# Layer 2's product with the squared adjacency: exact 12-bit halves in three single-pass products in place of Strassen's seven fp32 products

## The chip, the cores and the metric

The kernel runs on one core of one Trainium2 chip. The metric is the device time of one execution in microseconds (us). Engine names are those of the profile: PE (TensorE, with PEld for its weight loads), DVE (VectorE), ACT (ScalarE), POOL (GpSimd), SP (SyncE, which here only issues DMAs).

## The reference, cut to what matters

Four layers run one after the other on `x` (32 x 512 x 128, fp32), each as `x = x + layer(relu(layernorm(x)))`. Layer 2 is the one concerned:

```
weights  = coeff * A                       # both are adj: the squared adjacency, 512 x 512
features = relu(H @ psi_w + psi_b)         # H = relu(layernorm(x))
messages = einsum('nm,bnd->bmd', weights, features)
h        = relu(concat(messages, H) @ phi1_w + phi1_b)
x        = x + h @ phi2_w + phi2_b
```

The line `messages` is the product that the change rewrites: for each of the 32 batch entries, a 512 x 512 matrix (transposed) by a 512 x 128 one. Layer 0 (softmax attention), layer 1 (two Chebyshev hops) and layer 3 (tanh-limited attention masked by `adj`) stay as they are.

## The kernel before, in words

**Tiling.** Tokens lie in four blocks of 128 partitions (`NT` = 4). A *round* `q` handles two batch entries at once, so there are 16 rounds per layer (`NQ` = 16). All products are in fp32. One fp32 matmul in the program shows as two LDWEIGHTS and two MATMUL records in the trace: `p_score` is issued 128 times by the loops of lines 1089 to 1110 (16 rounds, two entries, four blocks) and has 256 records.

**The product with Strassen.** `mixed` (line 393) computes the product of the 512 x 512 matrix with the two entries of a round by a seven-product form of Strassen's scheme in which the two entries and the two halves of the token axis make the 2 x 2 blocks. Each of the seven products is `by_feature` (line 376): two matmuls that hold a 128 x 128 block of features and stream 256 columns of the matrix, so a round has 14 matmuls and 28 records. The left operands need three sums of the matrix's blocks, made once by `sum_steps` (line 301) and kept in a tile with the tag `sums` (two buffers). The right operands need four differences of 128 x 256 per round, made on POOL by `right_blocks` (line 338) in tiles of the tag `rt` (six buffers of 128 x 512). Three PSUM banks, a, c and d, take the products; two ACT copies and five DVE additions per round carry them out (lines 400 to 419).

**Layer 2.** `layer2(q)` (line 1053) is a generator whose parts are: normalise (ACT), transpose through DVE and a bounce in DRAM, one idle part, features (`p_feat` on PE, bias on DVE, Relu on ACT, then the right operands), the product `p_msgT` and four small POOL additions of `phi2b`, `p_phi`, and last `p_l2` with the addition into `x`. Its messages go to `msgT`.

**The squared matrix.** `square()` (line 1139) loads `adj` into the tile `sq` with its rows crossed, loads the transposed mask `adjTx` for layer 3, squares the four blocks on POOL with a copy back, and makes the block sums. `sq` and `adjTx` each take one of the four buffers of the tag `square`, which also hold `adj_s`, `x1T` and, in layer 3, the tiles `ex`.

**Order of the work.** Up to line 1157 (layer 0) the order on PE, DVE, ACT and POOL is as written. After it, the loop of lines 1166 to 1172 advances all active generators by one part per step, oldest first; a new round enters in each step. In one step PE thus gets, from the oldest round to the newest, `p_l2`, `p_phi`, `p_msgT` and `p_feat` of four neighbouring rounds. This order is the priority from which the framework's planner lays out each engine's queue and hands out buffers: an instruction whose tile has no free buffer is held back. Layer 1's last two pairs of rounds overlap layer 2's first rounds and use the same `rt` tiles; layer 2's last rounds overlap layer 3's first.

Of the kernel before, what the change touches and what calls it, by code (L numbers as in the profile page):

```python
# [8 lines left out]

F32 = mybir.dt.float32  # L10
F16 = mybir.dt.float16
BF16 = mybir.dt.bfloat16
AF = mybir.ActivationFunctionType
OP = mybir.AluOpType
AX = mybir.AxisListType

P = 128
QR = 32
NQR = P // QR
NEG = 9000000000000000.0  # L20
EPS = 1e-5


@with_exitstack
def kernel(
# [37 lines left out]
    nc = tc.nc  # L63
    B, N, D = x.shape
    NT = N // P
# [4 lines left out]
    const = ctx.enter_context(tc.tile_pool(name="const", bufs=1))  # L70
# [3 lines left out]
    work = ctx.enter_context(tc.tile_pool(name="work", bufs=4))  # L74
    bounce = ctx.enter_context(tc.tile_pool(name="bounce", bufs=4, space=bass.MemoryType.DRAM))

    def bank(name):
        return psum.tile([P, 512], F32, tag="bank", name=name)

# [7 lines left out]
    def square_tile(name):  # L87
        return const.tile([P, NT, N], F32, tag="square", name=name, bufs=4)

    def crossed(ap):  # L90

        return ap.rearrange("p (a b c) -> p b a c", a=NT, b=NQR)

    def split(ap):
        return ap.rearrange("p (a b c) -> p a b c", a=NT, b=NQR)

    def load_crossed(dst, src):
        for b in range(NQR):
            tc.keep_in_program_order(
                nc.sync.dma_start(dst[:, b, :], src.rearrange("(a b c) w -> b a c w", a=NT, c=QR)[b]))  # L100
# [91 lines left out]
    shift, scale = {}, {}  # L192
# [105 lines left out]
    H = N // 2  # L298
    sums = {}

    def sum_steps(mat, name, eng=nc.gpsimd):

        a11, a12 = mat[:, 0:2, 0:H], mat[:, 2:4, 0:H]
        a21, a22 = mat[:, 0:2, H:N], mat[:, 2:4, H:N]
        extra = const.tile([P, 3, 2, H], F32, tag="sums", name=f"sums_{name}", bufs=2)
        s1, s2, s4 = extra[:, 0], extra[:, 1], extra[:, 2]
        sums[name] = {1: a11, 2: a12, 3: s4, 4: a22, 5: s1, 6: s2, 7: a21}
        for out, op, p, q in ((s1, OP.add, a21, a22), (s2, OP.subtract, s1, a11),
                              (a21, OP.subtract, a11, a21), (s4, OP.subtract, a12, s2)):
            tc.keep_in_program_order(eng.tensor_tensor(out, p, q, op))  # L310
            yield
# [6 lines left out]
    def att_sums():  # L318

        a11, a12 = attT[:, 0:2, 0:H], attT[:, 2:4, 0:H]  # L320
        a21, a22 = attT[:, 0:2, H:N], attT[:, 2:4, H:N]
        extra = const.tile([P, 3, 2, H], F32, tag="sums", name="sums_att", bufs=2)
        s1, s2, s4 = extra[:, 0], extra[:, 1], extra[:, 2]
        sums["att"] = {1: a11, 2: a12, 3: s4, 4: a22, 5: s1, 6: s2, 7: a21}
        yield
        for out, p, bank_of, half, first in ((s1, a21, 2, 1, False), (s2, s1, 0, 0, False),
                                             (a21, a21, 0, 0, True), (s4, s2, 2, 0, True)):
            for k in range(2):
                b = pt[bank_of + k][:, half * H : half * H + H]
                if out is s1:  # L330
                    nc.vector.tensor_add(out[:, k], b, p[:, k])
                elif first:
                    nc.vector.tensor_sub(out[:, k], b, p[:, k])
                else:
                    nc.vector.tensor_sub(out[:, k], p[:, k], b)
            yield

    def right_blocks(half, name, engs):

        right = {}  # L340
        for _ in right_steps(half, name, engs, right):
            pass
        return right
# [21 lines left out]
    def products(name, form, left, right, evict, order=ORDER, on=lambda k, p: p):  # L365


        banks = {}
        for k, g, first in order:
            if first:  # L370
                banks[g] = bank(f"p_{name}_{g}")
            form(on(k, banks[g]), left[k], right[k], first)
            evict(k, banks[g])
            yield
# [18 lines left out]
    def mixed(name, left, right, dst):  # L393

        m1 = dst[:, 0, H:], dst[:, 1, :H], dst[:, 1, H:]

        def evict(k, p):
            p = p[:, :H]
            if k == 1:
                nc.scalar.copy(m1[0], p)  # L400
            elif k == 6:
                nc.vector.tensor_add(m1[1], p, m1[0])
            elif k == 7:
                nc.vector.tensor_add(m1[2], p, m1[0])
            elif k == 5:
                return
            elif k == 2:
                nc.scalar.copy(dst[:, 0, :H], p)
            elif k == 4:
                nc.vector.tensor_add(dst[:, 0, H:], p, m1[0])  # L410
            elif k == 3:
                nc.vector.tensor_add(dst[:, 1, :H], p, m1[1])

        def evict2(k, p):
            evict(k, p)
            if k == 5:
                held.append(p)
            if k == 7:
                nc.vector.tensor_add(dst[:, 1, H:], held[0][:, :H], m1[2])

        held = []
        return products(name, by_feature, left, right, evict2)

    def at(hT, b):
        return lambda t: hT[:, t, b, :]
# [90 lines left out]
    for t in range(NT):  # L516
        for s in range(t + 1):
            nc.tensor.matmul(pi[:, t : t + 1], upto[:, s, blk(t)], rch[:, s : s + 1],
                             start=(s == 0), stop=(s == t))

    p = bank("p_qk_t")
# [27 lines left out]
    parts = []  # L549
    for i in range(3):  # L550
        eh = prep.tile([P, NK], BF16, name=f"eh_{i}")
        nc.gpsimd.tensor_copy(eh, ecoln)
        part = prep.tile([P, NK], F32, name=f"part_{i}")
# [11 lines left out]
    for t in range(NT):  # L565
        s = prep.tile([P, NE], F16, tag="lt", name=f"lt_{t}", bufs=2)
# [3 lines left out]
        for j in range(NT):  # L570
            nc.tensor.matmul(pg[j // 2][:, j % 2, :], m[:, t, blk(j)], of_row[:, t, :],
                             start=(t == 0 and j % 2 == 0), stop=(t == NT - 1), skip_group_check=True)
    pb = bank("p_known")[:, : 2 * NK].rearrange("p (k e) -> p k e", e=2)
    for kk in range(NK):
        for t in range(NT):
            nc.tensor.matmul(pb[:, kk, :], of_row[:, t, blk(kk)], known[:, t, :],
                             start=(t == 0), stop=(t == NT - 1))
# [17 lines left out]
    for kk in range(NK):  # L595
        for j in range(NT):
            nc.tensor.matmul(pw[kk][:, j * P :], pgs[:, j, blk(kk)], upto[:, j, j * P :],
                             start=(j == 0), stop=(j == NT - 1), skip_group_check=True)
# [10 lines left out]
    for kk in range(NK):  # L609
        s = prep.tile([P, N], F16, tag="scr", name=f"scr_c{kk}", bufs=2)  # L610
# [88 lines left out]
    late = ctx.enter_context(tc.tile_pool(name="late", bufs=4))  # L699
# [338 lines left out]
    def layer1_stats():  # L1038

        ln_stats(NQ - 2)  # L1040
        yield
        ln_stats(NQ - 1)
# [10 lines left out]
    def layer2(q):  # L1053
        h = normed(q)
        yield
        hT = transposed(h, f"hT2_{q}")
        yield
        yield
        feat = []
        for b in range(2):  # L1060
            pf = projected(f"p_feat_{q}_{b}", (at(hT, b), psi))
            feat.append(late.tile([P, NT, D], F32, tag="hs", name=f"feat_{q}_{b}", bufs=6))
            nc.vector.tensor_add(feat[b], pf, spread(psib, NT))  # L1063
            nc.scalar.activation(feat[b], feat[b], AF.Relu)  # L1064
        right = right_blocks(lambda J, b: feat[b][:, 2 * J : 2 * J + 2, :], f"feat_{q}", [nc.gpsimd] * 4)
        yield
        if q % 2 == 0:
            msgs.append(quad_tile(f"msgT_{q}"))
        msgT = msgs[-1][:, q % 2, : 2 * N].rearrange("p (b w) -> p b w", b=2)
        for _ in mixed(f"msgT_{q}", sums["sq"], right, msgT):  # L1070
            pass
        for b in range(2):
            for i in range(0, NT, 2):
                xi = xt[q][:, b, i : i + 2, :]
                tc.keep_in_program_order(nc.gpsimd.tensor_add(xi, xi, spread(phi2b, 2)))  # L1075
        yield
        h1T = msgT
        for b in range(2):
            ph = bank(f"p_phi1_{q}_{b}")
            nc.tensor.matmul(ph, phi1[:, 1, :], hT[:, :, b, :], start=True, stop=False)  # L1080
            nc.tensor.matmul(ph, phi1[:, 0, :], msgT[:, b], start=False, stop=True)
            nc.scalar.activation(crossed(h1T[:, b]), split(ph), AF.Relu, bias=phi1b)
        yield
        for b in range(2):
            po = projected(f"p_l2_{q}_{b}", (columns(h1T[:, b]), phi2))
            nc.vector.tensor_add(xt[q][:, b], po, xt[q][:, b])
        ln_stats(q)
# [46 lines left out]
            if not final:  # L1134
                nc.sync.dma_start(out_r, xt[q][:, b])

    adjTx = []

    def square():

        sq = square_tile("sq")
        load_crossed(sq, adj)
        adjTx.append(square_tile("adjTx"))
        load_crossed(adjTx[0], adjT_d)
        yield
        for i in range(NT):
            s = late.tile([P, N], F32, tag="hs", name=f"sq_{i}", bufs=6)
            nc.gpsimd.tensor_mul(split(s), crossed(sq[:, i, :]), crossed(sq[:, i, :]))
            nc.gpsimd.tensor_copy(sq[:, i, :], s)
        yield from sum_steps(sq, "sq")  # L1150

    next_layer = layer1(0)
    for r in range(NQ // 2):
# [4 lines left out]
    waiting = [[next_layer, layer1(1), layer0_stats()]]  # L1158
# [3 lines left out]
    waiting[-1].append(layer2(0))  # L1162
    waiting += [[layer2(q)] for q in range(1, NQ)]
    waiting[-NQ + 7].append(layer1_stats())
    waiting += [[layer3(q)] for q in range(NQ)]
    active = []
    while waiting or active:
# [37 lines left out]
```

## Time and profile before

| | before |
|---|---|
| time, median of three (us) | 963.71 (963.55 to 964.28) |
| span of the profiled execution (us) | 961.7 |
| PE busy, records | 953.3 us (99%), 5465 |
| DVE busy | 584.4 us (61%) |
| ACT busy | 469.1 us (49%) |
| POOL busy | 423.8 us (44%) |
| DMA | 86.04 MB, mean 89 GB/s |

"Busy" is the union of the time in which an engine has an instruction in work. PE's matmuls overlap one another[...], so the duration of one record is longer than its share of PE: what a matmul costs a full PE is read from the distance between the *starts* of neighbouring records. The timeline gives, for a run of like records, the start of the first and their number, and so this distance.

The records of `p_msgT` run from 451.3 us to 670.2 us of the span. This is layer 2's stretch, and its first 20 us overlap layer 1.

### The profile page before, as it was taken

How to read it: one execution, taken by the hardware profiler on the slowest of the kernel's cores; microseconds unless marked ns; L12 is line 12 of the kernel's file. 1: busy time of each engine (PE TensorE's matmuls, PEld its weight loads, DVE VectorE, ACT ScalarE, POOL GpSimd, SP SyncE). 2: the span in 40 equal slices, each digit the busy share in tenths (PEclk: the TensorE clock that was granted, in tenths of full speed). 3: DMA queues.
4: the chain of work that ended last, by engine and by line, in shares of the span. 5: the costliest groups of instructions: out<-in, count | busy, mean ns of one | idle time of the engine just before them, and what ended most of it. 6: DMA issues, size and time to landing. Idle time of an engine off the chain costs nothing.

```text
span 961.7 us, 15152 instructions
## 1 busy us (share of the span) xinstructions
PE 953.3 (99%) x5465; PEld 780.8 (81%) x5465; DVE 584.4 (61%) x1326; ACT 469.1 (49%) x1054; POOL 423.8 (44%) x470
## 2 busy tenths in 40 slices
PE   8999999999999999999999999999999999999998
PEld 4899999898989999899877777777677777767776
DVE  8888885846536545656667665665654444444444
ACT  5865542442232233277627655444765445544553
POOL 5878987833517522513333444433032233223322
PEclk9999999999999999999999999999999999999999
DMA  9356532441341230343333433223121121211111
GB/s 252 62 166 185 160 108 84 104 110 55 102 136 45 66 88 23 110 110 96 89 99 97 126 91 85 74 82 88 56 88 56 55 77 44 72 61 45 55 33 44
DMA packets 83913, 86.04 MB, mean 89 GB/s; under 512 B 6784, under 2 KB 74624, under 8 KB 83840
## 3 DMA queue, kind: packets, MB, share of 16 engines
q1 hardware_dynamic: 83552, 84.57, 31.6%
q8 instruction: 43, 0.70, 0.3%
q10 hardware_dynamic: 288, 0.52, 0.2%
q14 instruction: 30, 0.25, 0.1%
HBM read 44.17 MB, written 40.89 MB: 88 GB/s over the span
## 4 chain that ended last, share of the span: by engine, by line
PE 96%; ACT 2%; DVE 1%; DMA 0%; POOL 0%; issue 0%; DVEq 0%; ACTq 0%
PE p_av L1125 12%; PE p_score L1110 11%; PE p_l_c L386 8%; PE p_w L435 6%; PE p_l_d L386 6%; PE p_msgT_c L379 5%; PE p_l_a L386 4%; PE p_x1T_c L379 4%; PE p_l L435 3%; PE p_feat L435 3%; PE p_hv L435 3%; PE p_qkh L1097 3%; PE p_x1T_a L379 3%; PE p_msgT_d L379 3%; PE p_g L435 3%; PE p_x1T_d L379 3%
## 5 line engine op out<-in xcount | busy, mean ns | idle before, releaser
L247 ACT ACTIVATE h<-x,sh,rs 128x128 f32<-128x128 f32 x512 | 209.2, 484 | 51.7 <-PE p_x1T_d L379 21.7
L1115 POOL TENSOR_TENSOR ex<-ex,adjTx 128x512 f32<-128x512 f32 x62 | 80.3, 1295 | 208.3 <-ACT ex L1113 202.8
L1111 ACT ACTIVATE ex<-p_score 128x512 f32<-128x512 f32 x128 | 71.9, 587 | 122.8 <-issue 113.0
L1125 PEld LDWEIGHTS p_av<-qkh_hv,ex 128*128 128x128 f32 x1024 | 118.4, 191 | 8.4 <-issue 7.4
L1125 PE MATMUL p_av<-qkh_hv,ex 128*128 128x129 f32 x1024 | 119.9, 274 | 0.0
L1110 PE MATMUL p_score<-qkh_hv,hT 128*128 128x512 f32 x256 | 115.2, 593 | 0.0
L283 DVE STREAM_TRANSPOSE hb_hT<-h 128x512 f32<-128x512 f32 x120 | 82.0, 698 | 23.7 <-ACT h L247 22.6
L1115 DVE TENSOR_TENSOR ex<-ex,adjTx 128x512 f32<-128x512 f32 x66 | 46.1, 703 | 82.0 <-ACT ex L1113 81.9
L227 DVE BATCH_NORM_STATS2 bn<-x 128x6 f32<-128x256 f32 x248 | 89.8, 419 | 0.6
L1110 PEld LDWEIGHTS p_score<-qkh_hv,hT 128*128 128x128 f32 x256 | 46.2, 190 | 46.5 <-issue 44.5
L1113 ACT ACTIVATE ex<-ex 128x512 f32<-128x512 f32 x128 | 76.7, 630 | 1.9
L356 POOL TENSOR_TENSOR rt_feat<-feat,feat 128x256 f32<-128x256 f32 x16 | 11.6, 725 | 136.4 <-ACT feat L1064 136.4
L958 ACT COPY w<-p_w 128x512 f32<-128x512 f32 x32 | 18.2, 574 | 106.1 <-PE p_w L435 106.1
L356 POOL TENSOR_TENSOR rt_w<-w,rt_w 128x512 f32<-128x512 f32 x16 | 20.4, 1273 | 110.3 <-DVE rt_w L356 92.0
L435 PE MATMUL p_w<-th,x1T 128*128 128x128 f32 x256 | 49.5, 275 | 0.0
L435 PE MATMUL p_w<-th,hs 128*128 128x128 f32 x256 | 49.5, 275 | 0.0
L435 PEld LDWEIGHTS p_hv<-vw,hT 128*128 128x128 f32 x256 | 33.6, 192 | 15.3 <-issue 8.1
L1075 POOL TENSOR_TENSOR x<-x,phi2b 128x256 f32<-128x256 f32 x64 | 44.5, 727 | 0.0
L435 PEld LDWEIGHTS p_w<-th,hs 128*128 128x128 f32 x256 | 39.9, 192 | 0.7
L1064 ACT ACTIVATE feat<-feat 128x512 f32<-128x512 f32 x32 | 20.1, 629 | 41.4 <-DVE feat L1063 41.4
L1130 DVE SCALAR_TENSOR_TENSOR x<-p_av,rsum,x 128x128 f32<-128x128 f32 x128 | 39.1, 347 | 1.9
L712 POOL TENSOR_TENSOR hd<-hT,adiag 128x512 f32<-128x512 f32 x32 | 39.6, 1274 | 0.2 <-ACT adiag L838 0.2
(238 smaller groups left out, 2039.7 us busy)
## 6 DMA issues: line engine op xcount, KB each, us to landing
d_hT<-hb_hT SPq DMA_DIRECT2D x240, 128.0 KB
hT<-d_hT SPq DMA_DIRECT2D x60, 512.0 KB
x<-in_x_dram SPq DMA_DIRECT2D x32, 256.0 KB
out_dram<-x SPq DMA_DIRECT2D x31, 256.0 KB
adjT_d<-adj_squares SPq DMA_DIRECT2D x4, 256.0 KB
sq<-in_adj_dram SPq DMA_DIRECT2D x4, 256.0 KB
adjTx<-adjT_d SPq DMA_DIRECT2D x4, 256.0 KB
adj_s<-in_adj_dram ACTq DMA_DIRECT2D x2, 256.0 KB
```

The costliest lines, as they stand in the source:

```text
L227: nc.vector.bn_stats(st[:, k].rearrange("p e s -> p (e s)"), xt[q][:, b, t : t + 2, :].rearrange("p t f -> p f t"))
L247: nc.scalar.activation(h[:, b, t, :], xt[q][:, b, t, :], AF.Relu, bias=shift[q][:, i : i + 1], scale=scale[q][:, i : i + 1])
L283: nc.vector.transpose(hb[:, :, b].rearrange("p j t r -> p t j r"), h[:, b].rearrange("p t (j c) -> p t j c", c=QR))
L379: nc.tensor.matmul(p[:, :H], b[:, k, :], a[:, k, :], start=(first and k == 0), stop=(k == 1), skip_group_check=True)
L386: nc.tensor.matmul(p[:, i * 2 * D : (i + 1) * 2 * D], a[:, k, blk(i)], b[:, k], start=(first and i == 0 and k == 0), stop=(k == 1), skip_g ...
L435: nc.tensor.matmul(p[:, blk(t)], hT(t), w, start=(i == 0), stop=(i == len(terms) - 1))
L1075: tc.keep_in_program_order(nc.gpsimd.tensor_add(xi, xi, spread(phi2b, 2)))
L1110: nc.tensor.matmul(ps, hT[:, t, b, :], qkh, start=True, stop=True)
L1111: nc.scalar.activation(ex[:, t, :], ps, AF.Tanh, scale=1.0 / (8.0 * math.sqrt(D)))
L1113: nc.scalar.activation(ex[:, t, :], ex[:, t, :], AF.Exp, scale=8.0)
L1115: eng.tensor_mul(split(ex[:, t, :]), split(ex[:, t, :]), crossed(adjTx[0][:, t, :]))
L1125: nc.tensor.matmul(po[:, i, : D + 1], ex[:, t, blk(i0 + i)], hv[:, t, :], start=(t == 0), stop=(t == NT - 1))
```

## The change

The seven products are replaced by three. A matrix `a` is split into `high`, its value rounded to a short significand (a write into the 32-bit type `float32r`, after a factor just under 1), and the rest. With the rest as `low` and a third part `mid` that combines both, the sum of three products of parts gives the full product. Each part is meant to be held exactly in 12 bits, so that a matmul on `float32r` operands can take it in a single pass. The three products are plain: all 512 columns of the matrix stream past each 128 x 128 block of the features, four blocks per product, for each of the two entries (24 matmuls per round). `near` collects high and low, `far` the mid part. ACT carries `near` out with a factor, and DVE adds `far`.

- `right_parts` splits the features of an entry: one pass of 128 x 512 each on ACT, POOL and DVE per entry, in place of the four POOL differences of 128 x 256 per round. It takes three `rt` tiles per entry, six per round, where the Strassen differences took two per round.
- `left_parts` splits the squared matrix once, block by block. `sq_high` and `sq_low` take two `square` buffers, and `sq_mid` one of `sums`, whose buffers grow from three to four parts.
- `square` now loads `adj` row block by row block through tiles of the tag `hs`, with a yield after each load and each block.
- The load of `adjTx` moves from `square` to `load_mask`, which enters with the last but one round of layer 2.

```diff
-        extra = const.tile([P, 3, 2, H], F32, tag="sums", name=f"sums_{name}", bufs=2)
+        extra = const.tile([P, 4, 2, H], F32, tag="sums", name=f"sums_{name}", bufs=2)
...
+    def left_parts(src, parts, i):
+        high, low, mid = (part[:, i, :] for part in parts)
+        nc.scalar.activation(high, src, AF.Copy, scale=DOWN)
+        nc.gpsimd.tensor_sub(src, src, high.bitcast(F32))
+        nc.scalar.activation(low, src, AF.Copy, scale=LOW)
+        nc.gpsimd.tensor_sub(mid, low.bitcast(F32), high.bitcast(F32))
+
+    def right_parts(src, name):
+        high, low, mid = (work.tile([P, NT, D], F32R, tag="rt", name=f"{part}_{name}", bufs=6)
+                          for part in ("high", "low", "mid"))
+        nc.scalar.activation(high, src, AF.Copy, scale=DOWN)
+        nc.gpsimd.tensor_sub(low, src, high.bitcast(F32))
+        nc.vector.scalar_tensor_tensor(mid, high.bitcast(F32), UP, src, OP.mult, OP.subtract)
+        return high, low, mid
+
+    def mixed_parts(name, left, right, dst):
+        near, far = bank(f"p_{name}_near"), bank(f"p_{name}_far")
+        for p, part in ((near, 0), (near, 1), (far, 2)):
+            for t in range(NT):
+                nc.tensor.matmul(p, right[part][:, t, :], left[part][:, t, :],
+                                 start=(t == 0 and part != 1), stop=(t == NT - 1 and part != 0))
+            if part == 1:
+                nc.scalar.activation(dst, near, AF.Copy, scale=UP)
+        nc.vector.tensor_add(dst, far, dst)
...
-        right = right_blocks(lambda J, b: feat[b][:, 2 * J : 2 * J + 2, :], f"feat_{q}", [nc.gpsimd] * 4)
+        right = [right_parts(feat[b], f"feat_{q}_{b}") for b in range(2)]
...
-        for _ in mixed(f"msgT_{q}", sums["sq"], right, msgT):
-            pass
+        for b in range(2):
+            mixed_parts(f"msgT_{q}_{b}", sq, right[b], msgT[:, b])
...
     def square():
-        sq = square_tile("sq")
-        load_crossed(sq, adj)
+        sq.extend(const.tile([P, NT, N], F32R, tag="square", name=f"sq_{part}", bufs=4) for part in ("high", "low"))
+        sq.append(const.tile([P, NT, N], F32R, tag="sums", name="sq_mid", bufs=2))
+        adj_b = adj.rearrange("(a b c) w -> b a c w", a=NT, c=QR)
+        for i in range(NT):
+            row = late.tile([P, N], F32, tag="hs", name=f"adj_{i}", bufs=6)
+            tc.keep_in_program_order(nc.sync.dma_start(row, adj_b[i]))
+            yield
+            s = late.tile([P, N], F32, tag="hs", name=f"sq_{i}", bufs=6)
+            nc.gpsimd.tensor_mul(split(s), crossed(row), crossed(row))
+            left_parts(s, sq, i)
+            yield
+
+    def load_mask():
+        yield
         adjTx.append(square_tile("adjTx"))
         load_crossed(adjTx[0], adjT_d)
-        yield
-        for i in range(NT):
-            s = late.tile([P, N], F32, tag="hs", name=f"sq_{i}", bufs=6)
-            nc.gpsimd.tensor_mul(split(s), crossed(sq[:, i, :]), crossed(sq[:, i, :]))
-            nc.gpsimd.tensor_copy(sq[:, i, :], s)
-        yield from sum_steps(sq, "sq")
...
+    waiting[-2].append(load_mask())
```

More of the change, by code (lines that the diff above doesn't have):

```diff
@@ L10 @@
 F32 = mybir.dt.float32
+F32R = mybir.dt.float32r
 F16 = mybir.dt.float16
@@ L21 @@
 EPS = 1e-5
+LOW = 4096.0
+DOWN = 1.0 - 1.0 / 8192.0
+UP = 1.0 + 1.0 / 4096.0
 @with_exitstack
@@ L321, in att_sums @@
         a21, a22 = attT[:, 0:2, H:N], attT[:, 2:4, H:N]
-        extra = const.tile([P, 3, 2, H], F32, tag="sums", name="sums_att", bufs=2)
+        extra = const.tile([P, 4, 2, H], F32, tag="sums", name="sums_att", bufs=2)
         s1, s2, s4 = extra[:, 0], extra[:, 1], extra[:, 2]
@@ L1135, in layer3 @@
                 nc.sync.dma_start(out_r, xt[q][:, b])
-    adjTx = []
+    adjTx, sq = [], []
     def square():
-        sq = square_tile("sq")
-        load_crossed(sq, adj)
+        sq.extend(const.tile([P, NT, N], F32R, tag="square", name=f"sq_{part}", bufs=4) for part in ("high", "low"))
[11 more added lines that the diff above has]
+        yield
         adjTx.append(square_tile("adjTx"))
         load_crossed(adjTx[0], adjT_d)
-        yield
-        for i in range(NT):
-            s = late.tile([P, N], F32, tag="hs", name=f"sq_{i}", bufs=6)
-            nc.gpsimd.tensor_mul(split(s), crossed(sq[:, i, :]), crossed(sq[:, i, :]))
-            nc.gpsimd.tensor_copy(sq[:, i, :], s)
-        yield from sum_steps(sq, "sq")
     next_layer = layer1(0)
```

## The prediction

> **What bounds the kernel now.** I began with the page's first two parts, the busy times and the slices.
>
> ```profile
> PE 953.3 (99%) x5465; PEld 780.8 (81%) x5465; DVE 584.4 (61%) x1326; ACT 469.1 (49%) x1054; POOL 423.8 (44%) x470
> ...
> PE   8999999999999999999999999999999999999998
> ```
>
> PE is busy in every slice, and no other engine is over 61%. The share alone doesn't say that PE streams all the time, so next came the chain of work that ended last:
>
> ```profile
> PE 96%; ACT 2%; DVE 1%; DMA 0%; POOL 0%; issue 0%; DVEq 0%; ACTq 0%
> ```
>
> 96% of the way back from the end is PE itself. What is taken from PE comes off the time one for one, as long as nothing else takes the place. What the product costs on PE is seen in the timeline of PE over one round of layer 2:
>
> ```profile
> 610.69 1.03 PE L379 MATMUL p_msgT_a<-sq,feat 128*128 128x256 f32 x4
> 611.56 1.03 PE L379 MATMUL p_msgT_c<-sums_sq,rt_feat 128*128 128x256 f32 x4
> 612.42 1.03 PE L379 MATMUL p_msgT_d<-sums_sq,rt_feat 128*128 128x256 f32 x4
> 613.41 1.13 PE L379 MATMUL p_msgT_c<-sq,rt_feat 128*128 128x256 f32 x4
> 614.38 1.03 PE L379 MATMUL p_msgT_a<-sq,feat 128*128 128x256 f32 x4
> ...
> 616.97 1.95 PE L435 MATMUL p_feat<-psi,hT 128*128 128x128 f32 x16
> 618.75 1.95 PE L435 MATMUL p_l<-phi,msgT 128*128 128x128 f32 x16
> 620.54 1.02 PE L1080 MATMUL p_phi<-hT,phi 128*128 128x512 f32 x2
> ...
> 623.98 1.03 PE L379 MATMUL p_msgT_a<-sq,feat 128*128 128x256 f32 x4
> ```
>
> Columns: start, length, engine and line, names, shapes, number of records. Four records take 611.56 - 610.69 = 0.865 us, that is 0.216 us each. The 28 records of the product take 616.97 - 610.69 = 6.28 us: 28 x 0.216 = 6.05, and two small gaps (0.99 instead of 0.865 before 613.41, 0.97 before 614.38), together 0.23 us. The whole round is 623.98 - 610.69 = 13.29 us: product 6.28, `p_feat` 1.78, `p_l` 1.79, `p_phi` 3.44. Last, what the product's prepared operands wait for, in the view of the tile `rt_feat`:
>
> ```profile
>   ACT feat L1064: 136.4, 16
>   DVE msgT L402: 4.5, 12
> ```
>
> POOL idles before each of the 16 rounds, because features come late, not because POOL is full. The second line shows what the small gaps are: in 12 rounds a PSUM bank is freed by DVE just too late.
>
> **What the Trainium skill says.** "FP8 and Floating Point Precision", TensorE Precision Notes: true FP32 takes four passes, while the reduced-precision way reads the 4-byte value, truncates it and multiplies natively. The trace agrees with the four: one fp32 matmul of 256 columns is 2 x 0.216 = 0.432 us, and 4 x 256 columns at the page's 2.4 GHz are 0.427. No record of before is of the reduced kind. "TensorE: Matmul & The Clock Gate", Back-to-back issue gap, prices an isolated pass at N/2.4 + 2.5 ns, so 0.216 us for 512 columns. Before has bf16 matmuls of that width, and they agree (6 in 21.29 - 20.00 = 1.29 us, 0.215 each):
>
> ```profile
> 20.00 1.46 PE L635 MATMUL p_val<-at_part,at_row 128*128 128x512 bf16 x6
> 21.29 0.59 PE L631 MATMUL p_later<-at_col,at_row 128*128 128x512 bf16 x2
> ```
>
> The same page, LDWEIGHTS, puts a load at columns/1.2, so 107 ns. Here a 4-byte load lasts 0.19 us, but 16 of them pass in 1.97 us (0.12 each) under `p_feat`, so one per 0.216 us is hidden. And in its section on the array it calls ACT and DVE strict FIFOs: an instruction that waits holds what is queued behind it.
>
> **The change part by part.**
>
> *The product on PE.* 24 matmuls of 512 columns replace 28 records. The cost of one `float32r` record is not in the trace. From below it is one pass, 0.216 us (the bf16 row); from above it is what a fp32 record of that width takes, `p_phi`, 3.44/8 = 0.430 us, since each fp32 record streams two cycles a column. I take 0.216, since the count of four passes fits the measured fp32 matmul to 1%, and a reduced operand needs one. A round's product is then 24 x 0.216 = 5.18 us, and 16 rounds give 16 x (6.05 - 5.18) = 13.9 us. The two gaps should go as well: `near` takes eight matmuls without an eviction in between, and `far` has its own bank. 12 rounds x 0.23 = 2.8 us. PE gains 16.7 us.
>
> *Evictions.* ACT loses two copies of 128x256 (0.357 + 0.369) and gets two of 128x512 (0.58, the row of `w<-p_w`). DVE loses five additions of 0.42 = 2.10 us and gets two of 0.69 = 1.38. `p_phi` reads the messages only after `p_feat` and `p_l` of neighbouring rounds, 3.6 us of PE work; the last addition ends under 1 us after the last matmul. At nothing.
>
> *Splitting the features.* Per round: ACT two more copies at 0.63 (the row of Relu on `feat`), POOL two subtractions at 1.27 in place of four at 0.727 (2.54 for 2.91), DVE two `scalar_tensor_tensor` at 0.68 to 0.80 (the two rows of line 996; I take 0.80). Sums per round: ACT +1.70, DVE +0.88, POOL -0.37 us. In 600 to 680 us, the undisturbed part of layer 2, ACT is busy 38.2 and DVE 47.5 of 80 us, so 6.3 and 7.9 of a round of 13.29. They become 8.0 and 8.8 of 12.2: 66% and 72%. Neither bounds.
>
> The new waits: `low` on POOL and `mid` on DVE wait for `high` on ACT, which waits for the Relu. Behind `mid` on DVE stand the additions of `p_l` and layer 1's or 2's statistics; behind `high` on ACT the next Relu and the normalisation of a round three steps ahead, which no one needs yet. From the end of `p_feat`'s first entry to its use lies the second entry (0.9), `p_l` (1.79) and `p_phi` (3.44), 6.1 us. The chain is DVE bias 0.69 + Relu 0.63 + `high` 0.63 + `low` 1.27 = 3.2 us, up to 5 with some 0.2 to 0.4 us of hand-over at each step and one foreign instruction in the way. `low` is wanted only four matmuls later still. Hidden in the steady state.
>
> *Buffers.* A round now needs all six `rt` tiles, where it took two. In the steady state a round's tiles are free once its product has run, before the next is split. Where layer 1's last pairs overlap, four tiles of `rt_w` and six of parts must take turns: pair 6's products, round 0, pair 7's, round 1. After three such turns one chain of about 3 us may be bare, though PE has `p_w` (7 us between 436 and 451) and others to put there. I charge 2 us; bounds 0 and 10.
>
> *Once.* Squaring: POOL 4 x 1.15 + 8 x 1.27 = 14.8 us against 4 x 1.15 + 4 x 0.72 + 4 x 1.27 = 12.6; ACT + 8 x 0.63 = 5 us; spread over nine steps of layer 1, where POOL is at half. `adjTx` is 1 MB, fetched two rounds before its use at 26% DMA share, into a buffer left by layer 1. Both at nothing.
>
> Sum: 963.7 - 13.9 - 2.8 + 2 = 949.0 us.
>
> **The rivals.**
> - *The preparation takes part of it back.* For it: the six buffers all used, a chain through three strict queues, and the loads of `adj` through `hs` in SP's queue, ahead of other rounds' transfers. Against: PE has at least 5 us of other work in each round. Three bare turns at 3.2 us, and nothing of the small gaps gained: 963.7 - 13.9 + 9.6 = 959.4.
> - *A `float32r` record streams two cycles a column.* For it: the fp32 transposes in layer 0 (`p_hT`, eight in 23.89 - 23.02 = 0.87 us, one record each) take 0.109 us for 128 columns, twice a pass, so 4-byte operands may be fed at half rate. Against: a transpose has to carry all 32 bits. Then 384 x 0.430 = 165.1 against 96.8 + 2.8: 963.7 + 65.5 = 1029, slower.
> - *The chain is bare in every round*, by 2 us, because `mid` is stuck in DVE behind statistics: 949 + 32 = 981, slower. Against it stand the 6.1 us.
>
> **How the numbers follow.** My forecast 0.70, partly taken back 0.17, two cycles 0.08, bare each round 0.05. The forecast reaches from 945 (no loss at the turns, and a little more regained) to about 954; of the second case most lies below 961, and a fifth or so (0.03) within 0.2% of before. The range 945 to 961 thus leaves out the two slow cases and that fifth. Faster 0.70 + 0.14 = 0.84, same 0.03, slower 0.13.
>
> **What would show it.** Records of `p_msgT` 0.216 us apart, 384 of them; a steady round of 12.2 us; no gap in PE before `near` or `far`; ACT and DVE at about 66% and 72% there. PE idle before the first rounds of layer 2 would show the turns of the `rt` tiles. A distance of 0.43 us would refute the step "a reduced operand needs one pass"; a wait on `low` or `mid` in the list of PE's waits would refute "hidden".

## The result, and the profile after

| | before | after |
|---|---|---|
| time, median (us) | 963.82 (963.55 to 964.28) | 968.62 (967.46 to 969.72) |
| ratio to before, 95% interval | | 1.005 (1.0036 to 1.0064) |
| span of the profiled execution (us) | 961.7 | 966.6 |
| PE busy (us) | 953.3 | 945.7 |

The change is slower by 4.8 us, where 14.7 us of gain were forecast. The page of the changed kernel, busy times and slices:

```profile
PE 945.7 (98%) x5401; PEld 771.1 (80%) x5401; DVE 602.1 (62%) x1310; ACT 496.9 (51%) x1094; POOL 436.8 (45%) x438
...
PE   8999999999996999999999999999999999999998
...
PEclk9999999999998999999999999999999999999999
```

PE is busy for 7.6 us less, and yet the span is longer. The 13th slice has a 6 where PE stood at 9 before, and the granted clock dips beside it. The chain that ended last says the same; it was 96% PE before:

```profile
PE 79%; POOL 9%; issue 6%; DMA 2%; DVE 2%; ACT 2%; POOLq 0%; DVEq 0%
```

The list of PE's waits (who waited for whom, total us, times, longest) names the place:

```profile
PE p_x1T_c L383 <- DVE x1T L406: 12.1, 4, 8.7
...
PE p_msgT_near L453 <- POOL low_feat L444: 0.7, 1, 0.7
```

`p_x1T` is layer 1's product, which the diff doesn't touch. Before, this wait (line 402 there) came to 0.2 us. What the change was about, the product `p_msgT`, has one wait of 0.7 us in 16 rounds. A round of layer 2 in the timeline of PE:

```profile
605.89 1.02 PE L1116 MATMUL p_phi<-msgT,phi 128*128 128x512 f32 x2
606.35 1.50 PE L453 MATMUL p_msgT_near<-sq_high,high_feat 128*128 128x512 f32 x4
607.68 1.10 PE L453 MATMUL p_msgT_near<-sq_low,low_feat 128*128 128x512 f32 x4
608.61 1.10 PE L453 MATMUL p_msgT_far<-sq_mid,mid_feat 128*128 128x512 f32 x4
609.55 1.09 PE L453 MATMUL p_msgT_near<-sq_high,high_feat 128*128 128x512 f32 x4
...
612.34 1.95 PE L470 MATMUL p_feat<-psi,hT 128*128 128x128 f32 x16
...
618.95 1.49 PE L453 MATMUL p_msgT_near<-sq_high,high_feat 128*128 128x512 f32 x4
```

Four records take 608.61 - 607.68 = 0.93 us, so 0.233 us each, and the groups follow one another without a gap. (The first `near` record starts under the last `p_phi` record, whose pair takes 0.86 us elsewhere; so the product has 612.34 - 606.75 = 5.59 us, which is 24 x 0.233.) The round is 618.95 - 606.35 = 12.60 us, against 13.29 before. Layer 2 did become faster. Added up over the 16 rounds, from the first record to what follows, the products took 99.9 us before and take 90.8 now, a gain of 9.1 us. Twelve rounds take 5.57 to 5.60 us; four take 5.67, 6.52, 5.84 and 5.67, and in the last three of these a group of `low` is late. The loss lies in layer 1, around 300 us, where the squared matrix is split. PE's timeline there:

```profile
300.64 1.03 PE L383 MATMUL p_x1T_d<-sums_adj,rt_h 128*128 128x256 f32 x4
310.40 2.07 PE L383 MATMUL p_x1T_c<-adj_s,rt_h 128*128 128x256 f32 x4 [8.73 <-DVE x1T L406]
312.27 1.66 PE L383 MATMUL p_x1T_a<-adj_s,h 128*128 128x256 f32 x4
313.76 1.03 PE L383 MATMUL p_x1T_c<-adj_s,rt_h 128*128 128x256 f32 x4
```

PE stands still for 8.73 us. The eight records after it take 313.76 - 310.40 = 3.36 us instead of 8 x 0.216 = 1.73, so 1.6 us more are lost to a slow clock. The Trainium skill, "TensorE: Matmul & The Clock Gate", Part 1, says that an idle window of about 3.4 us drops the PE clock to half until it has been busy as long; the trace agrees: the mean granted clock is 0.53 in these 3.36 us, and 1.00 in 320 to 340 us. DVE's addition of line 406 waits for ACT's copy of line 404, and ACT's timeline shows why that is late:

```profile
299.58 0.63 ACT L436 ACTIVATE sq_low<-sq 128x512 fp32r<-128x512 f32 x1 [2.31 <-POOL sq L435]
300.12 0.57 ACT L993 COPY w<-p_w 128x512 f32<-128x512 f32 x1
300.58 0.50 ACT L237 ACTIVATE sd<-bn,eps 128x8 f32<-128x8 f32 x2
307.00 0.63 ACT L434 ACTIVATE sq_high<-sq 128x512 fp32r<-128x512 f32 x1 [5.92 <-POOL sq L1184]
307.53 0.57 ACT L993 COPY w<-p_w 128x512 f32<-128x512 f32 x1
309.00 0.63 ACT L436 ACTIVATE sq_low<-sq 128x512 fp32r<-128x512 f32 x1 [0.90 <-POOL sq L435]
309.53 0.35 ACT L404 COPY x1T<-p_x1T_a 128x256 f32<-128x256 f32 x1
```

The copy of line 404, whose matmuls were done by about 300 us, stands in ACT's queue behind `sq_high` and `sq_low` of the second block. These wait for POOL, and POOL waits for the row of `adj`:

```profile
305.93 1.04 POOL L1184 TENSOR_TENSOR sq<-adj 128x512 f32<-128x512 f32 x1 [4.37 <-DMA adj<-in_adj_dram]
```

That load was issued at 300.23 us and landed 5.56 us later. What held the issue is in SyncE's timeline, and in the list of its waits:

```profile
300.23 0.57 SPq L1181 DMA_DIRECT2D adj<-in_adj_dram  x1
```

```profile
SPq L1181 <- ACT w L993: 7.8, 1, 7.8
```

The issue had waited 7.8 us, in the end for ACT: its copy `w` stood behind the first block's `sq_low`, which had waited 2.31 us for POOL and ended at 300.21 us, just before the issue. So the row is late in part because ACT's queue was blocked already. Two of the other three waits, at 348.77 (1.58 us) and 385.67 (1.63 us), have the same chain from the row on.

### The profile page after: what moved, and what is told of

Its sections match the earlier page's. It is cut to its first block, busy times and chain, and to the rows that moved or that the text cites. A ratio compares the mean times of both kernels' runs of the same rounds, so it can differ in the third digit from the quotient of the medians.

```text
span 966.6 us, 15066 instructions
## 1 busy us (share of the span) xinstructions
PE 945.7 (98%) x5401; PEld 771.1 (80%) x5401; DVE 602.1 (62%) x1310; ACT 496.9 (51%) x1094; POOL 436.8 (45%) x438
## 4 chain that ended last, share of the span: by engine, by line
PE 79%; POOL 9%; issue 6%; DMA 2%; DVE 2%; ACT 2%; POOLq 0%; DVEq 0%
PE p_av L1160 12%; PE p_score L1145 11%; PE p_l_c L390 6%; PE p_w L470 4%; PE p_x1T_c L383 4%; PE p_msgT_near L453 4%; PE p_l_d L390 4%; PE p_l_a L390 3%; PE p_hv L470 3%; PE p_qkh L1132 3%; PE p_x1T_a L383 3%; PE p_x1T_d L383 3%; PE p_msgT_far L453 2%; PE p_g L470 2%; PE p_l L470 2%
## 5 line engine op out<-in xcount | busy, mean ns | idle before, releaser
L444 POOL TENSOR_TENSOR low_feat<-feat,high_feat 128x512 fp32r<-128x512 f32 x32 | 52.6, 1658 | 119.4 <-ACT high_feat L443 114.1
L237 ACT ACTIVATE sd<-bn,eps 128x8 f32<-128x8 f32 x62 | 18.5, 304 | 61.6 <-DVE bn L231 54.6
L1110 POOL TENSOR_TENSOR x<-x,phi2b 128x256 f32<-128x256 f32 x64 | 47.8, 778 | 0.0
L383 PE MATMUL p_x1T_c<-adj_s,rt_h 128*128 128x256 f32 x128 | 34.9, 396 | 12.1 <-DVE x1T L406 12.1
L453 PE MATMUL p_msgT_near<-sq_high,high_feat 128*128 128x512 f32 x128 | 40.8, 440 | 0.0
```

Of the source, the lines that this page charges most:

```text
L383: nc.tensor.matmul(p[:, :H], b[:, k, :], a[:, k, :], start=(first and k == 0), stop=(k == 1), skip_group_check=True)
L453: nc.tensor.matmul(p, right[part][:, t, :], left[part][:, t, :], start=(t == 0 and part != 1), stop=(t == NT - 1 and part != 0))
```

## The experiments

My theory after the result: PE is held through ACT's queue, by work of the squaring that waits for POOL, and with the late rows as the root. Rivals: POOL or the loads alone hold PE; or the chain of the splitting does so whether rows are late or not.

**Rows early.** The changed kernel, with the four blocks of `adj` loaded together into a free `quad` tile, one step before the first is squared:

```diff
-        for i in range(NT):
-            row = late.tile([P, N], F32, tag="hs", name=f"adj_{i}", bufs=6)
-            tc.keep_in_program_order(nc.sync.dma_start(row, adj_b[i]))
-            yield
+        rows = quad_tile("adj_rows").rearrange("p w e -> p (w e)")[:, : 4 * N].rearrange("p (t w) -> p t w", t=NT)
+        for i in range(NT):
+            tc.keep_in_program_order(nc.sync.dma_start(rows[:, i, :], adj_b[i]))
+        yield
+        for i in range(NT):
+            row = rows[:, i, :]
             s = late.tile([P, N], F32, tag="hs", name=f"sq_{i}", bufs=6)
```

> The changed kernel with one edit: the four row blocks of adj are loaded together, one step before the first is squared, into a free quad tile instead of one by one through hs tiles. Theory (late rows: POOL waits in order for a row that was issued late and takes 5.5 us to land, ACT's sq_high and sq_low wait behind it, and the x1T eviction behind those holds PE): PE's 12.1 us of waits on DVE x1T L406 go below 2 us, with them about 2 us of slow PE clock; 953 to 957 us. Rival (the splitting chain itself, ACT to POOL to ACT, is what delays the eviction, whenever the row is there): the waits stay above 8 us; 964 to 969 us.

Measured: 962.88 us, ratio to before 0.9993 (0.9985 to 1.0002). PE's waits there:

```profile
PE p_x1T_c L383 <- DVE x1T L406: 6.4, 2, 6.2
```

This is neither number. With no row missing, 6.4 of the 12.1 us stay, all but 0.2 in one wait, at 307.74 us. ACT's timeline shows the queue once more, now with two blocks' parts ahead of the copy:

```profile
305.85 0.63 ACT L436 ACTIVATE sq_low<-sq 128x512 fp32r<-128x512 f32 x1 [0.42 <-POOL sq L435]
306.39 0.57 ACT L993 COPY w<-p_w 128x512 f32<-128x512 f32 x1
306.85 0.38 ACT L404 COPY x1T<-p_x1T_a 128x256 f32<-128x256 f32 x1
```

So the late row is part of the cause, not its root: POOL's own queue (here `rt_h`, `hs` and the splitting of two blocks) is enough to hold ACT. The edit also takes out a `yield` per block, so that blocks follow one step apart and not two, and two of them meet here; how much of the 6.4 us one block alone would leave isn't shown.

**The row loads alone.** The kernel before, with Strassen, and the squares made from rows that are loaded as in the change:

```diff
         sq = square_tile("sq")
-        load_crossed(sq, adj)
         adjTx.append(square_tile("adjTx"))
         load_crossed(adjTx[0], adjT_d)
-        yield
+        adj_b = adj.rearrange("(a b c) w -> b a c w", a=NT, c=QR)
         for i in range(NT):
+            row = late.tile([P, N], F32, tag="hs", name=f"adj_{i}", bufs=6)
+            tc.keep_in_program_order(nc.sync.dma_start(row, adj_b[i]))
+            yield
             s = late.tile([P, N], F32, tag="hs", name=f"sq_{i}", bufs=6)
-            nc.gpsimd.tensor_mul(split(s), crossed(sq[:, i, :]), crossed(sq[:, i, :]))
+            nc.gpsimd.tensor_mul(split(s), crossed(row), crossed(row))
             nc.gpsimd.tensor_copy(sq[:, i, :], s)
+            yield
```

> The kernel before (Strassen) with the row by row loading of the change alone: each block of adj through an hs tile, squared and copied into sq on POOL in the step after; nothing of it on ACT. If a late row needs ACT to reach PE (theory): POOL waits for rows, PE idles under 3 us more than before; 964 to 967 us. If POOL's wait alone reaches PE through rt_h or hs (rival): 970 to 976 us.

Measured: 963.47 us, ratio 0.9999 (0.9991 to 1.0008), and PE waits as before (0.2 us on `x1T`). Row by row loading costs nothing by itself. What was missing for a loss is work on ACT that waits for it. But a row as late as in the changed kernel was not tested here: the second load was issued at 295.25 us and not at 300.23, and POOL waited 1.24 us at most for a row, where it waited 4.37 there.

**The squared matrix's parts on POOL.** The changed kernel, rows still loaded late, without the two ACT instructions per block:

```diff
-        nc.scalar.activation(high, src, AF.Copy, scale=DOWN)
+        nc.gpsimd.tensor_scalar(high, src, DOWN, None, OP.mult)
         nc.gpsimd.tensor_sub(src, src, high.bitcast(F32))
-        nc.scalar.activation(low, src, AF.Copy, scale=LOW)
+        nc.gpsimd.tensor_scalar(low, src, LOW, None, OP.mult)
```

> The changed kernel, rows loaded late as there, but sq_high and sq_low made on POOL instead of ACT, so that ACT holds nothing that waits for a row. Theory (ACT's queue carries the wait to PE): the waits of p_x1T_c on DVE L406 fall from 12.1 to under 3 us; 955 to 960 us. Rival (POOL alone carries it): they stay; 966 to 972 us.

Measured: 954.25 us in a single execution. Timed again:

> The kernel of e3_left_pool again, timed: sq_high and sq_low made on POOL, all else as in the change. PE's share of the gain is then 99.9 us (records of p_msgT before, first to next start) less 384 x 0.233 = 89.5 us, so 10 us if nothing else is lost: 953 to 955 us. If the single look was luck: 957 us or more.

Measured: 954.49 us (before on the same chip: 963.93), ratio 0.9908 (0.9892 to 0.9925). Its waits of PE:

```profile
PE p_msgT_near L453 <- POOL low_feat L444: 0.6, 1, 0.6
...
PE p_x1T_c L383 <- DVE x1T L406: 0.2, 1, 0.2
```

and ACT at the place where it stood still (the copy of line 404 follows its own matmuls by 0.28 us):

```profile
298.98 0.59 ACT L993 COPY w<-p_w 128x512 f32<-128x512 f32 x1
299.85 0.37 ACT L404 COPY x1T<-p_x1T_a 128x256 f32<-128x256 f32 x1 [0.28 <-PE p_x1T_a L383]
```

The wait is back to what it was before the change, although POOL has more to do (448.8 us busy instead of 436.8; one part costs it 1.49 us, where ACT took 0.63) and the loads stand at the same place of the program. In time the second one comes earlier, though: its issue waits for PE alone, at 295.40 us, and POOL doesn't wait for that row. So this run shows that the stop goes with the two instructions on ACT, but it doesn't part ACT's queue from the late row; the next one does. This version is faster than both kernels.

**What stands behind.** The changed kernel with its parts on ACT, and layer 1's first eviction moved to DVE:

```diff
             if k == 1:
-                nc.scalar.copy(m1[0], p)
+                nc.vector.tensor_copy(m1[0], p)
```

> The changed kernel, sq_high and sq_low on ACT as there, but layer 1's first eviction x1T (line 404) moved from ACT to DVE, so that the first thing that PE waits for no longer stands behind sq_low. Theory (what matters is what stands behind the waiting instruction on ACT): the waits of PE on DVE x1T L406 fall from 12.1 to under 2 us; the copies w and the second eviction still stand behind, so PE may wait up to 4 us on those; 955 to 960 us. Rival (ACT's queue is not the carrier): the waits stay above 8 us; 966 to 970 us.

Measured: 961.46 us in a single execution; the waits on line 406 are 5.0 us in five pieces. The second row is as late here as in the changed kernel (issued at 300.27 us, and POOL waits 4.08 us for it). The two longest waits, in the timeline of PE:

```profile
302.61 1.13 PE L383 MATMUL p_x1T_c<-adj_s,rt_h 128*128 128x256 f32 x4 [0.90 <-DVE x1T L406]
312.31 2.08 PE L383 MATMUL p_x1T_c<-adj_s,rt_h 128*128 128x256 f32 x4 [2.96 <-DVE x1T L406]
314.18 1.06 PE L383 MATMUL p_x1T_a<-adj_s,h 128*128 128x256 f32 x2
```

The stop of 8.73 us has shrunk to 0.90 with POOL and ACT held as before, as the theory has it: ACT's queue is what carries the wait to PE. But the fall is not to under 2 us in all, and the time is 1.5 us over what I had named: `sq_low` at 308.76 us now holds ACT's second eviction and four normalisations, DVE's transpose (311.23 us) waits for those, and the next addition of line 406 stands behind the transpose. Moving one instruction out of a blocked queue passes the wait on by the next one. Taking the blocking instruction out ends it.

**The price of a `float32r` record.** The changed kernel with all parts in bf16 (rounded to 8 bits, so the product loses precision; the casts that go with it are left out here):

```diff
-        high, low, mid = (work.tile([P, NT, D], F32R, tag="rt", name=f"{part}_{name}", bufs=6)
+        high, low, mid = (work.tile([P, NT, D], BF16, tag="rt", name=f"{part}_{name}", bufs=6)
...
-        sq.extend(const.tile([P, NT, N], F32R, tag="square", name=f"sq_{part}", bufs=4) for part in ("high", "low"))
+        sq.extend(const.tile([P, NT, N], BF16, tag="square", name=f"sq_{part}", bufs=4) for part in ("high", "low"))
```

> The changed kernel with all six parts (high, low, mid, left and right) held in bf16: the parts are rounded to 8 bits, so the product loses precision; all else as in the change. Measures the distance between neighbouring records of p_msgT, 0.233 us with float32r. If the extra 17 ns over the 0.216 us of a 512-column pass belong to the 4-byte operands: 0.216. If they belong to the place (traffic of the other engines, alternating weights): 0.23. The stalls in layer 1 should be as in the change, so about 962 to 966 us with the first, 968 with the second.

Measured: 962.40 us in a single execution, with 10.8 us of the same waits in layer 1. The distance is 0.216 us:

```profile
604.07 1.03 PE L453 MATMUL p_msgT_near<-sq_low,low_feat 128*128 128x512 bf16 x4
604.93 1.03 PE L453 MATMUL p_msgT_far<-sq_mid,mid_feat 128*128 128x512 bf16 x4
```

And the POOL version with each matmul cut into two of 256 columns:

```diff
-                nc.tensor.matmul(p, right[part][:, t, :], left[part][:, t, :],
-                                 start=(t == 0 and part != 1), stop=(t == NT - 1 and part != 0))
+                for c in (slice(0, H), slice(H, N)):
+                    nc.tensor.matmul(p[:, c], right[part][:, t, :], left[part][:, t, c],
+                                     start=(t == 0 and part != 1 and c.start == 0),
+                                     stop=(t == NT - 1 and part != 0), skip_group_check=True)
```

> e5_left_pool_timed with each float32r matmul of 512 columns cut into two of 256, so 768 records. A pass of 256 columns is 0.109 us. If the extra of 17 ns is a fixed cost of each float32r record: 0.126 us from record to record, a product of 6.05 us per round, 960 to 962 us. If it grows with the columns (8%): 0.117 to 0.118 us, 5.65 us per round, 954 to 956 us. If both records are held by the weight loads, the loads' spacing will show it.

Measured: 955.83 us in a single execution. Eight records take 609.20 - 608.26 = 0.94 us, so 0.1175 each:

```profile
608.26 1.10 PE L454 MATMUL p_msgT_far<-sq_mid,mid_feat 128*128 128x256 f32 x8
609.20 1.10 PE L454 MATMUL p_msgT_near<-sq_high,high_feat 128*128 128x256 f32 x8
```

The extra over the pass goes with the 4-byte operands and grows with the columns, 8% over a bf16 pass of 512 columns, and about as much over a two-byte pass of 256 (four fp16 records of `p_row` in the kernel before take 12.35 - 11.91 = 0.44 us, 0.11 each); a fixed 17 ns would have given 0.126. What in the feeding of the array causes it is open; no run told the streamed operand from the stationary one.

## Why the prediction was wrong

- *PE bounds the kernel, and what is taken from it comes off one for one*: right. With the stall gone, the products give 9.1 us (90.8 in that run too, against 99.9) and the time shows 9.4 (963.93 - 954.49).
- *"At nothing" for squaring, once*: **this step failed.** It added up POOL's and ACT's work, found POOL at half, and put the waits between the two at nothing. But a share doesn't tell what an instruction holds up while it waits. I had named what stands behind the waiting instructions of layer 2, not behind those of `left_parts`: ACT waits twice per block for POOL, and behind it in the queue are the evictions of `x1T`, whose banks PE needs at once. It cost 11.9 us of PE's idle time (12.1 less the 0.2 that is there anyway) and 1.6 us of slow clock after the longest stop. This makes 13.5 of the 14.2 us by which the change and the POOL version lie apart (968.62 - 963.82 against 954.49 - 963.93); 0.7 us are not assigned.
- *"A reduced operand needs one pass, 0.216 us"*: the mechanism was right (one record, no half rate), but the term was mis-sized: 0.233 us. 384 x 0.017 = 6.5 us less gain than worked out. (The 2.4 GHz in the working of the four passes is a figure of the TensorE page, which the prediction names next, not of the page on precision; the sum stands.)
- *The small gaps go*: right for those that were there. New ones came in three rounds, where a group of `low` is late.
- *Splitting the features is hidden*: right but for about 1.3 us. The list has one wait of 0.7 us in 16 rounds, and three products are longer by 0.93, 0.25 and 0.08 us. By the prediction's own sign, a wait on `low` in that list, it isn't wholly hidden. In 600 to 680 us ACT is busy 50.8 and DVE 60.0 of 80 us, 64% and 75%, where I had 66% and 72%. POOL's `low` takes 1.73 us (median) and not 1.27; there was room for it.
- *Buffers*: charged with 2 us for bare turns of the `rt` tiles; no PE wait on them beyond those 0.7 us is seen, so too much.
- *The rivals.* The slow ones, two cycles a column and a chain bare in each round, didn't come true, though the time is slower. "The preparation takes part of it back" had the right family, but its reasons (the six buffers, other transfers behind the loads of `adj` in SP's queue) aren't the ones. I had bounded it at 9.6 us for three turns, which gave 959.4, and the range ended at 961; one blocked queue took 13.5.

With what the products really gave, with the stall put in and the 2 us for buffers left out, the sum is 963.8 - 9.1 + 13.5 = 968.2; measured 968.6.

## What to carry to other kernels

When a change adds a small one-time job that passes between two engines, list what is queued behind each of its waiting instructions in the stretch where it runs, also if that stretch belongs to another layer: an eviction behind a wait stops PE, however idle that engine is on average (here ACT, busy for half of the span). Keep a job that waits for POOL and DMA on an engine on which nothing that PE needs soon stands behind it: here one longer POOL chain was 14 us better than a shorter one shared with ACT. And read a new operand type's price from a run before summing hundreds of it: 8% on 384 records was 6.5 us.

## What the runs showed of the hardware that was not expected

- A `float32r` matmul of 512 columns follows the one before by 0.233 us, of 256 by 0.1175 us; bf16 in the same place takes 0.216. The count of passes was right, and the time per column is 8% longer.
- POOL's subtraction `low` (two 128x512 inputs in SBUF) took 1.73 us in the median, and DVE's `mid`, from the same inputs at the same time, 0.68 to 1.75 us. Two of the 32 `low` (at 475.48 and 482.06 us) ran with no `mid` beside them and took 1.27 and 1.28; POOL's like subtraction into `sq_mid` took 1.27. The Trainium skill, "Advanced Engine Details and Errata", VectorE Performance Modes, says that DVE's second port is shared with GpSimd. The durations fit; that it is the port, and not something else in running side by side, is argued only.
- One stop of 8.73 us costs PE 1.6 us more, as the eight records behind it run at about half the clock. The three shorter stops there, 1.63 us at most, show no such tail. But in the run with the eviction on DVE a stop of 2.96 us was enough: its next four records took 314.18 - 312.31 = 1.87 us instead of 0.86, and the granted clock was 0.58 from 312.31 to 315.70 us. So a stop shorter than the 3.4 us that the page names can cost the clock too.
